# The end of a two-layer recurrent and attention kernel, put in another order

## The chip, the cores and the metric

The program runs on one core of a Trainium2 chip. A core has a matrix engine (PE; its weight loads are shown apart as PEld), a vector engine (DVE), an activation engine (ACT), a general engine (POOL), a queue engine (SP) and 16 DMA engines that they share. Every engine works through its own instructions strictly in the order in which the program holds them, and waits on semaphores for the others. The metric is the device time of one execution in microseconds (us); a smaller time is better. The program is the same for every input, so there are no data-dependent loops.

## The reference, cut to what matters

All arrays are float32. The input x has 8 batches of 512 tokens with 128 channels.

```python
xn = layernorm(x)
s  = L0_attn(xn)     # state-space scan (256 channels, 16 states), MLP with gelu, two rmsnorms
g  = silu(L0_ffn(xn))  # 24 experts, top 2 of 24, capacity 86, two layers, layernorm
x  = x + s * g       # called x1 below
xn = layernorm(x)
s  = L1_attn(xn)     # causal softmax attention, 8 heads of 128, per batch
g  = silu(L1_ffn(xn))  # 128 experts of 128x128, top 2, capacity 32 over ALL tokens
return x + s * g
```

Two things of it set the end of the program. The capacity of an expert of the second layer is counted over all 4096 tokens in order, so that the slots of the last batch are known only when its x1 is known, and the combined outputs are fetched by row numbers that the routing worked out. And `s * g` needs, for a batch, both the sum over its 8 heads and the experts' rows of its tokens.

## The kernel before, in words

The kernel is one Python function that records instructions for a scheduling layer. The layer gives each recorded instruction a place in its engine's list: an instruction that was recorded earlier goes first where it is ready in the layer's own plan of the run, and a later one may be pulled ahead of it. Buffers come from named pools with a fixed number of slots; a tile takes a slot of its tag when an older tile of that tag is done with, and slots are handed out in the order of recording. The order on each engine is therefore fixed when the program is built, and it need not be the order of the Python code.

Work of the first layer: `mixture` (24 experts, two passes) runs beside the first part of `model`, which is the state-space layer, batch after batch. `scan` (L651) is its inner part: per two states and half of the channels a product, two scans and a product on DVE (L665, L667, L668), fed by exponentials on ACT (L663), and eight transposes on PE (L689) that add into `py`. `back` (L723) ends a batch: gated output, projection, `rms`, transposes L745, gelu MLP (L751, L752, L756), second `rms`, and a store of the batch's s to DRAM (L763). 64 `step`s make up `model`.

Work of the second layer, per batch b:
- `fetch(b)` (L578) loads xn, s (L583) and x and adds two gathered rows of the first layer's experts per token;
- `after(b)` (L598) makes x1 from them: a layernorm, four elementwise operations (L605, L606, L608, L609, on POOL but for batch 0) and a store (L610);
- `prepare(b)` (L810) normalises x1 and makes `xaT`, the transposed input of attention;
- `choose(b)` and `route(b)` (L832, L856) make the logits, the top 2 and the slots, and scatter the batch's rows to DRAM in 8 indirect DMAs on POOL (L896);
- `heads(b)` (L962) yields after each of the 8 heads: `probabilities` of the next head (q product L914, four score products L922, masked minimum on DVE L924, exponential on ACT L928) and then `values` of this one (transposes L942, copies L944, products with v L949, and the scaled sums on DVE, L954 and L960). `values_of` (L900) makes v for four heads.

64 heads are to be done. 48 of them (EARLY = 6 batches) are recorded beside `model`, in one loop that advances both at the same pace, with `fetch`, `after`, `prepare` and `choose` of batch b+1 at heads 1, 3 and 4 of batch b. They share a PSUM pool of two slots, tag "pm", with `model`.

What follows is the end. The pools of the model are closed, new PSUM pools are opened (`ps_x`, `ps_q`), and a second Attention object works on them. `after`, `prepare` and `choose` of batch 7 are recorded, then `weights2` and `places` (which need the routing of all batches), and then a loop over the 16 heads of batches 6 and 7 with other work between them:

```python
    for _ in late():
        for f in second.pop(0) if second else []:
            f()
```

`second` holds the second layer's experts, 8 parts of 16 experts (`slots` loads and transposes the scattered rows, L1022 and L1025; `experts` multiplies, L1041, and stores, L1043 and L1044), one part beside a head, and then one `finish` beside each further head. `load_experts` (L1032) has eight buffers. `finish(b)` (L1046) loads the sum of the heads and x1 back from DRAM, gathers two rows per token from the experts' outputs (`gather`, 8 indirect DMAs of 128 rows per batch, six row buffers), weights and adds them on DVE (L1058, L1059), applies silu on ACT (L1060), multiplies, adds (L1061, L1062) and stores the output (L1063). No gather can start before the last expert's rows are stored, because every row of the table may be fetched.

Of the kernel before, what the change touches and what calls it, by code (L numbers as in the profile page):

```python
# [47 lines left out]
def tile_kernel(ctx: ExitStack, tc: tile.TileContext, t: dict, out: bass.AP):  # L48
# [528 lines left out]

    def fetch(b):  # L578
# [3 lines left out]
        sb = af.tile([P, NJ, D], F32, name="sb")  # L582
        Q.dma_start(sb, rows(s_dram[b][:, :]))  # L583
# [139 lines left out]
    def back(b, yt):  # L723
# [39 lines left out]
        Q.dma_start(rows(s_dram[b][:, :]), xo)  # L763
# [38 lines left out]
    class Attention:  # L802
# [129 lines left out]
        def values(self, hd, prob, v, s1):  # L932
# [12 lines left out]
            for i0 in range(0, NJ, 2):  # L945
# [9 lines left out]
                for i in range(i0, i0 + 2):  # L955
                    so, r = s1[:, i, :], rs[:, i - i0 : i - i0 + 1]
                    if hd == 0:
                        V.tensor_scalar(so, po[:, i - i0, 0:D], r, None, ALU.mult)
                    else:
                        V.scalar_tensor_tensor(so, po[:, i - i0, 0:D], r, so, ALU.mult, ALU.add)  # L960
# [71 lines left out]
    def load_experts(e0):  # L1032
        we = mo.tile([P, 8, D], F32, name="we3", bufs=8)
# [12 lines left out]
    def finish(b):  # L1046
        s1 = mo.tile([P, NJ, D], F32, name="s1f")
        Q.dma_start(s1, rows(s1_dram[b][:, :]))
        x1 = mo.tile([P, NJ, D], F32, name="x1f")
        Q.dma_start(x1, rows(x1_dram[b][:, :]))  # L1050
        y = mo.tile([P, NJ, D], F32, name="y", tag="y")
        for j in range(NJ):
            i = b * NJ + j
            ya = mo.tile([P, D], F32, name="ya", tag="row", bufs=6)
            yc = mo.tile([P, D], F32, name="yc", tag="row", bufs=6)
# [3 lines left out]
            V.scalar_tensor_tensor(y[:, j, :], yc, w121[:, i, 1:2], ya, ALU.mult, ALU.add)  # L1059
# [18 lines left out]
    def model():  # L1078
# [6 lines left out]
        for b in range(B):  # L1085
# [9 lines left out]
            for k in range(DS // NC):  # L1095
# [7 lines left out]
                if k == 6:  # L1103
# [44 lines left out]
    beside = Attention(at, m_qk, w_vo, pm, pm, (ps_s, "ps"), (ps_t, "pt"), (ps_o, "po"))  # L1148

    EARLY = 6  # L1150

    xb = after(0, *got)
    step()
    ready = {0: beside.prepare(0, xb)}
    step()

    def early():
        for b in range(EARLY):
            for hd, _ in enumerate(beside.heads(b, ready[b])):
                if hd == 0 and b == 0:  # L1160
                    beside.choose(0)
                if hd == 1:
                    got = fetch(b + 1)
                if hd == 3:
# [129 lines left out]
```

## Time and profile before

Three runs took 1581.38, 1583.21 and 1586.12 us. The profiled execution took 1584.26 us, with 1582.6 us between its first and last instruction. Stages of its end, times from the start of that span:

| us | what ends it | PE busy | DVE busy | ACT busy | POOL busy |
|---|---|---|---|---|---|
| 1296.0 to 1343.8 | transposes L745 of the last batch's `back` start | 41.2 of 47.8 | 29.4 | 23.1 | 8.1 |
| 1343.8 to 1359.5 | s of batch 7 is stored (L763) | 14.2 of 15.7 | 4.7 | 8.2 | 1.3 |
| 1359.5 to 1419.4 | first expert product (L1041) | 56.2 of 59.9 | 41.5 | 36.3 | 10.5 |
| 1419.4 to 1469.4 | last expert rows leave (L1044) | 45.9 of 50.0 | 27.8 | 14.3 | 0.0 |
| 1469.4 to 1572.9 | sum of batch 7's heads is stored (L977) | 62.6 of 103.5 | 50.5 | 45.1 | 61.8 |
| 1572.9 to 1582.6 | end | 0.0 of 9.7 | 1.4 | 0.0 | 0.0 |

A row is read as: in this stretch the engine executed something for so many us. An engine near the length of the stretch sets its pace; where none is near, the engines wait for each other or for DMAs. Over the whole span PE is busy 77% and DVE 78%; from 850 to 1300 us DVE is busy 95% of the time.

### The profile page before, as it was taken

The numbers are of one execution on the slowest core, as the hardware profiler recorded it, in microseconds if no ns is written. First come the engines' busy times: TensorE is split into PE (matmuls) and PEld (weight loads), VectorE is DVE, ScalarE is ACT, GpSimd is POOL, SyncE is SP. The second block draws the span as 40 slices with busy tenths as digits, with TensorE's granted clock in tenths as the row PEclk, the third lists the DMA queues.
The fourth block names the chain that finished last, engine by engine and source line by source line (L and its number), as shares of the span: only waits on it lengthen the run. The fifth ranks groups of instructions, "written<-read, shape, count | busy, mean of one in ns | idle before, by whom it ended". The sixth has DMA issues, their size and how long they took to land.

```text
span 1582.6 us, 20556 instructions
## 1 busy us (share of the span) xinstructions
PE 1223.6 (77%) x6793; PEld 859.4 (54%) x6793; DVE 1238.0 (78%) x2789; ACT 972.1 (61%) x1670; POOL 590.2 (37%) x501
## 2 busy tenths in 40 slices
PE   6878898213479898457998998789799898998655
PEld 4534454113367777444576755655566576567434
DVE  5687677788946867888899999999899985575454
ACT  5356776675648676565768578477575764642352
POOL 1166562656155433664343025252500302020564
PEclk9689899655689999777999999999999899999876
DMA  6577677777477764543132223232311200529233
GB/s 182 184 225 265 227 240 248 239 246 225 142 216 224 223 207 142 141 110 88 57 99 68 79 84 81 78 87 58 85 63 54 94 8 20 154 71 255 71 100 90
DMA packets 170220, 218.83 MB, mean 138 GB/s; under 512 B 16618, under 2 KB 117562, under 8 KB 170114
## 3 DMA queue, kind: packets, MB, share of 16 engines
q1 hardware_dynamic: 126018, 99.39, 20.5%
q10 hardware_dynamic: 18432, 67.12, 12.5%
q0 software_dynamic: 25664, 51.01, 12.0%
q8 instruction: 54, 0.88, 0.2%
q14 instruction: 52, 0.43, 0.1%
HBM read 161.56 MB, written 55.84 MB: 137 GB/s over the span
## 4 chain that ended last, share of the span: by engine, by line
DVE 37%; PE 29%; issue 10%; DMA 9%; ACT 7%; POOL 5%; another core or an unknown queue 2%; SPq 1%; DVEq 0%; ACTq 0%; POOLq 0%
DVE u L667 11%; DVE u L668 5%; PE po L949 4%; DVE u L665 4%; PE sc L922 4%; DVE sc L924 3%; PE py L689 2%; PE po L574 2%; DMA hd<-hs_dram,row 2%; PE pp L942 2%; DVE s L960 2%; PE ph L505 2%; PE pc L621 2%; POOL o L132 2%
## 5 line engine op out<-in xcount | busy, mean ns | idle before, releaser
L667 DVE TENSOR_TENSOR_SCAN u<-da,u 128x512 f32<-128x512 f32 x256 | 310.2, 1233 | 63.5 <-ACT da L663 54.6
L689 PE MATMUL py<-ident,u 128*128 128x128 f32 x1024 | 164.1, 301 | 158.1 <-DVE u L668 156.4
L689 PEld LDWEIGHTS py<-ident,u 128*128 128x128 f32 x1024 | 130.5, 155 | 203.5 <-DVE u L668 184.4
L949 PE MATMUL po<-v,pT 128*128 128x129 f32 x1280 | 188.1, 291 | 20.3 <-DVE s L960 11.4
L922 PE MATMUL sc<-xaT,qm 128*128 128x128 f32 (+3 forms) x512 | 182.0, 462 | 26.3 <-ACT prob L928 24.6
L663 ACT ACTIVATE da<-dt,a_neg 128x512 f32<-128x512 f32 x256 | 176.8, 720 | 38.9 <-DVE u L667 33.1
L949 PEld LDWEIGHTS po<-v,pT 128*128 128x128 f32 x1280 | 170.9, 203 | 53.0 <-issue 31.6
L928 ACT ACTIVATE prob<-sc,mn 128x128 f32<-128x128 f32 (+3 forms) x256 | 130.4, 527 | 99.3 <-DVE mn L924 82.5
L665 DVE TENSOR_TENSOR u<-bb,lp 128x1024 f32<-128x1024 f32 x128 | 154.5, 1229 | 13.8 <-DMA bb<-xd_dram 9.8
L668 DVE TENSOR_TENSOR u<-u,cb 128x1024 f32<-128x1024 f32 x128 | 156.2, 1220 | 1.2
L924 DVE CUSTOM_DVE_ANT_0 sc<-sc,mask 128x128 f32<-128x128 f32 (+3 forms) x256 | 124.3, 495 | 34.7 <-PE sc L922 28.0
L942 PE MATMUL pp<-ident,prob 128*128 128x128 f32 x640 | 113.1, 288 | 43.0 <-DVE pT L944 22.1
L942 PEld LDWEIGHTS pp<-ident,prob 128*128 128x128 f32 x640 | 80.3, 147 | 100.6 <-issue 44.6
L132 POOL DMA_INDIRECT o<-os_dram,row x60 | 103.3, 1722 | 79.6 <-DMA o<-xn_dram 32.8
L896 POOL DMA_INDIRECT xs_dram<-xn,idx x64 | 79.1, 1236 | 129.8 <-DVE row L893 50.8
L129 POOL DMA_INDIRECT xg<-xn_dram,inv x72 | 97.0, 1347 | 80.5 <-PE px L498 48.9
L129 POOL DMA_INDIRECT hg<-hid_dram,inv x72 | 89.8, 1247 | 99.5 <-PE pht L569 72.3
L922 PEld LDWEIGHTS sc<-xaT,qm 128*128 128x128 f32 x512 | 83.0, 196 | 68.8 <-ACT prob L928 43.9
L129 POOL DMA_INDIRECT hd<-hs_dram,row x64 | 80.0, 1249 | 72.0 <-DMA qkv_w<-in_qkv_w 23.8
L944 ACT COPY pT<-pp 128x384 f32<-128x384 f32 (+1 forms) x105 | 54.0, 514 | 70.9 <-PE pp L942 49.6
L574 PEld LDWEIGHTS po<-we,hgT 128*128 128x128 f32 (+1 forms) x576 | 72.5, 191 | 25.4 <-issue 20.5
L574 PE MATMUL po<-we,hgT 128*128 128x128 f32 (+1 forms) x576 | 81.2, 289 | 1.9 <-ACT hgT L571 1.8
(307 smaller groups left out, 2518.6 us busy)
## 6 DMA issues: line engine op xcount, KB each, us to landing
bb<-xd_dram ACTq DMA_DIRECT2D x64, 512.0 KB
cb<-xd_dram ACTq DMA_DIRECT2D x64, 512.0 KB
we<-in_W SPq DMA_DIRECT2D x48, 256.0 KB
hs_dram<-hs SPq DMA_DIRECT2D x24, 512.0 KB
hid_dram<-hd SPq DMA_DIRECT2D x32, 256.0 KB
we<-in_we SPq DMA_DIRECT2D x16, 512.0 KB
hs_dram<-hs SPq DMA_DIRECT2D x24, 192.0 KB
xb<-in_x SPq DMA_DIRECT2D x16, 256.0 KB
```

The lines of the kernel that those rows point to most:

```text
L129: G.indirect_dma_start(dst, None, table[:, :], IOA(idx, 0))
L132: G.indirect_dma_start(dst, None, table[:, :], IOA(idx, 0), compute_op=ALU.add)
L574: T.matmul(po[:r, c, :], hT[:, f, :r], we[:, f, :], start=False, stop=(f == NJ - 1))
L663: S.activation(da[:, j, :], dt[:, hf, :], AF.Exp, scale=a_neg[:, hf, n0 + j : n0 + j + 1])
L665: V.tensor_tensor(u, bb, bc(dx[:, hf : hf + 1, :], (P, NC, L)), ALU.mult)
L667: V.tensor_tensor_scan(u[:, j, :], da[:, j, :], u[:, j, :], 0.0, ALU.mult, ALU.add)
L668: V.tensor_tensor(u, u, cb, ALU.mult)
L689: T.matmul(py[:, i, hf * P : (hf + 1) * P], us[hf][:, j, i * P : (i + 1) * P], ident, is_transpose=True, start=False, stop=(n0 + j == DS - ...
L922: T.matmul(sc[:, :w], qm[:, i * P : w], xaT[:, :w], start=True, stop=True)
L924: V.tensor_tensor_reduce(sc[:, :w], sc[:, :w], mask[:, L - w :], -1.0, FMAX, ALU.add, ALU.min, mn[:, i : i + 1])
L942: T.transpose(pp[:, c, :], prob[i][:, k * P : (k + 1) * P], ident)
L949: T.matmul(po[:, i - i0, :], pT[:, i * (i + 1) // 2 + k, :], v[:, k, hd % 4, :], start=(k == 0), stop=(k == i),)
```

## The change

Seven edits, all of the end or leading to it.

1. 46 instead of 48 heads are recorded beside the model (`MODEL`), all by one generator over all 64 heads and with one Attention object, whose pools are replaced later.
2. `fetch(6)`, `after(6)`, `prepare(6)` and `choose(6)` move to heads 0, 1 and 2 of batch 5, and `fetch(7)` to its head 4, without s.
3. s of batch 7 is not stored and loaded again: the tile stays in SBUF (`last_s`), and L608 and L609 of batch 7, with L605 and L606, run on DVE in place of POOL.
4. `after`, `prepare` and `choose` of batch 7 are recorded right after the model, still in the model's pools; then six heads (`FILL`, numbers 46 to 51 counted from 0); then the pools are changed.
5. All 8 parts of the experts are recorded in one go; `load_experts` has six buffers in place of eight.
6. `finish` is split: `begin_finish` records loads and gathers with buffers for three batches; the weighting follows. The 12 heads left are recorded with a `finish` after each from the third on; the weighting is held behind the latest head's sums (`follows`). For batches 6 and 7 the load of the heads' sum stays in the second half.
7. The gate of the last batch's state-space output is computed at step 2 of its 8 steps, not at step 6.

```diff
@@ fetch, after, back @@
+    last_s = []
-        sb = af.tile([P, NJ, D], F32, name="sb")
-        Q.dma_start(sb, rows(s_dram[b][:, :]))
+        sb = None
+        if b < B - 1:
+            sb = af.tile([P, NJ, D], F32, name="sb")
+            Q.dma_start(sb, rows(s_dram[b][:, :]))
...
-        E = G
+        E = V if b in (0, B - 1) else G
         if o2 is not None:
-            E = V
             V.tensor_tensor(o, o, o2, ALU.add)
+        sb = last_s[0] if sb is None else sb
...
-        Q.dma_start(rows(s_dram[b][:, :]), xo)
+        if b < B - 1:
+            Q.dma_start(rows(s_dram[b][:, :]), xo)
+        else:
+            last_s.append(xo)
@@ values: both forms of the scaled sum are kept as self.summed @@
@@ load_experts @@
-        we = mo.tile([P, 8, D], F32, name="we3", bufs=8)
+        we = mo.tile([P, 8, D], F32, name="we3", bufs=6)
@@ finish @@
+    def begin_finish(b):
+        s1 = mo.tile([P, NJ, D], F32, name="s1f", bufs=3)
+        if b < B - 2:
+            Q.dma_start(s1, rows(s1_dram[b][:, :]))
+        x1 = mo.tile([P, NJ, D], F32, name="x1f", bufs=3)
+        Q.dma_start(x1, rows(x1_dram[b][:, :]))
+        yr = mo.tile([P, NJ, 2, D], F32, name="yr", bufs=3)
+        for j in range(NJ):
+            for k in range(2):
+                gather(yr[:, j, k, :], yb_dram, row1[:, b * NJ + j, k : k + 1])
+        return s1, x1, yr
+
+    def finish(b, s1, x1, yr):
+        if b >= B - 2:
+            Q.dma_start(s1, rows(s1_dram[b][:, :]))
...
-            gather(ya, yb_dram, row1[:, i, 0:1])
-            gather(yc, yb_dram, row1[:, i, 1:2])
-            V.tensor_scalar(ya, ya, w121[:, i, 0:1], None, ALU.mult)
-            V.scalar_tensor_tensor(y[:, j, :], yc, w121[:, i, 1:2], ya, ALU.mult, ALU.add)
+            ya = yr[:, j, 0, :]
+            weighted = V.tensor_scalar(ya, ya, w121[:, i, 0:1], None, ALU.mult)
+            follows(weighted, att.summed)
+            V.scalar_tensor_tensor(y[:, j, :], yr[:, j, 1, :], w121[:, i, 1:2], ya, ALU.mult, ALU.add)
@@ model @@
-                if k == 6:
+                if k == (6 if b < B - 1 else 2):
                     zsb = gate(xT)
@@ heads beside the model @@
     EARLY = 6
+    MODEL = 8 * EARLY - 2
+    FILL = 6
...
+    def all_heads():
+        for b in range(B):
+            late = b == EARLY - 1
+            for hd, _ in enumerate(att.heads(b, ready[b])):
...
+                if b < EARLY:
+                    if hd == (0 if late else 1):
+                        got = fetch(b + 1)
+                    if hd == (1 if late else 3):
+                        xb = after(b + 1, *got)
+                    if hd == (2 if late else 4):
+                        ready[b + 1] = att.prepare(b + 1, xb)
+                        att.choose(b + 1)
+                    if hd == 4 and late:
+                        last_got.append(fetch(B - 1))
...
     for _ in model_steps:
         pass
-    for _ in attention_steps:
-        pass
+    ready[B - 1] = att.prepare(B - 1, after(B - 1, *last_got[0]))
+    att.choose(B - 1)
+    for i in range(FILL):
+        next(attention_steps)
     psc.close()
     ssm.close()
@@ the end @@
-    for b in range(EARLY + 1, B):
-        ready[b] = last.prepare(b, after(b, *fetch(b)))
-        last.choose(b)
...
+    slots(0)
+    for t16 in range(E1 // 16):
+        for e0 in (16 * t16, 16 * t16 + 8):
             if e0 + 32 < E1:
                 loaded[e0 + 32] = load_experts(e0 + 32)
             experts(e0, loaded[e0])
...
         if t16 + 1 < E1 // 16:
-            second[-1].append(lambda t16=t16: slots(t16 + 1))
...
+            slots(t16 + 1)
+
+    begun = [begin_finish(b) for b in range(3)]
+    for i, _ in enumerate(attention_steps):
+        if 2 <= i < B + 1:
+            finish(i - 2, *begun[i - 2])
+            if i + 1 < B:
+                begun.append(begin_finish(i + 1))
+    finish(B - 1, *begun[B - 1])
```

More of the change, by code (lines that the diff above doesn't have):

```diff
@@ L957, in values @@
                     if hd == 0:
[L958 removed]
+                        self.summed = V.tensor_scalar(so, po[:, i - i0, 0:D], r, None, ALU.mult)
                     else:
[L960 removed]
+                        self.summed = V.scalar_tensor_tensor(so, po[:, i - i0, 0:D], r, so, ALU.mult, ALU.add)
         def heads(self, b, xaT):
```

49 lines of the change are left out of this document (8 added, 41 removed).

## The prediction

> **What bounds the kernel now.** I read, in this order, the table of stretches, the waits of the last stage, the order in time of SP and POOL around the last batch, and then, for each engine, the order in which the built program issues its instructions, before and after. Stretches of before (start:end, length, busy us and instructions of PE, PEld, DVE, ACT, POOL, granted clock, DMA share, GB/s):
>
> ```profile
> 1296.00:1343.80 47.80, 41.15 (x265) 31.69 (x263) 29.43 (x108) 23.07 (x47) 8.07 (x10) 1.00 0.04 12
> 1343.80:1359.50 15.70, 14.16 (x55) 7.61 (x56) 4.72 (x13) 8.19 (x18) 1.26 (x1) 1.00 0.07 18
> 1359.50:1419.40 59.90, 56.22 (x309) 38.17 (x307) 41.52 (x176) 36.30 (x68) 10.52 (x11) 1.00 0.49 130
> 1419.40:1469.40 50.00, 45.93 (x436) 36.44 (x436) 27.78 (x67) 14.34 (x27) 0.00 (x0) 0.97 0.82 230
> 1469.40:1572.90 103.50, 62.63 (x273) 45.35 (x271) 50.52 (x176) 45.10 (x68) 61.75 (x64) 0.77 0.31 89
> ```
>
> Up to 1469 PE is the bound, 92 to 94% busy from 1359 on: the chain of the last batch costs nothing there, because heads fill it. From 1469 nothing is busy over 61%. That stage is a convoy of 64 gathers, whose waits are:
>
> ```profile
> POOL ya L129 <- DMA yb_dram<-yb: 59.6, 1, 59.6
> ACT prob L928 <- DVE mn L924: 20.7, 5, 7.3
> DVE rsum L954 <- remote: 19.3, 3, 8.6
> PEld sc L922 <- ACT prob L928: 16.2, 4, 7.8
> POOL ya L129 <- DVE y L1059: 9.0, 4, 5.7
> ```
>
> The first line is POOL idle for 59.6 us until the last expert row is stored. Then it issues a gather each 1.25 us; the first starts 3.1 us after the last store (1469.4 to 1472.5). The chain of the last batch, SP first, then POOL:
>
> ```profile
> 1359.45 0.36 SPq L763 DMA_DIRECT2D s_dram<-xnb  x1
> 1361.90 3.96 SPq L1034 DMA_DIRECT2D we<-in_we  x4
> 1365.90 1.74 SPq L583 DMA_DIRECT2D sb<-s_dram  x1
> ...
> 1572.93 0.36 SPq L977 DMA_DIRECT2D s_dram<-s  x1
> 1575.22 0.36 SPq L1048 DMA_DIRECT2D s1f<-s_dram  x1
> 1579.27 0.38 SPq L1063 DMA_DIRECT2D out<-y  x1
> ```
>
> ```profile
> 1372.38 1.27 POOL L608 TENSOR_TENSOR o<-o,sb 128x512 f32<-128x512 f32 x1 [26.15 <-DMA sb<-s_dram]
> 1373.73 1.27 POOL L609 TENSOR_TENSOR xb<-o,xb 128x512 f32<-128x512 f32 x1
> 1402.64 1.01 POOL L896 DMA_INDIRECT xs_dram<-xn,idx  x1 [27.64 <-DVE idx L890]
> ```
>
> s goes out at 1359.45, its reload is issued behind four weight loads and lands at 1372.38, x1 is ready at 1375.0, the slots at 1402.6, the scatters end at 1412.9.
>
> **A price list for PE**, in us per instruction of the program, from rows such as fourteen L949 records (seven instructions) in 1.73 and 32 L1041 records (16) in 1.90: L949 0.25, L942 0.155, L922 0.63 (mean of four widths), L914 and L907 1.0, L1025 0.15, L1041 0.119; one head 8.6. Multiplied with the order of before it gives 76.7 for 1343.8 to 1419.4 (75.6 measured) and 46.5 for the experts (50.0 measured, the rest waits for rows). So it may be used on the order of after.
>
> **1. Up to the last batch's `back` (L745; 1343.8 before).** 47 heads instead of 48 lie in front of it on PE, 7.6 us less by the list; DVE has 8.1 us less before L740. The new order has 17 more activation-table loads on ACT (85 for 68 up to the last exponential of the scan), 1.283 us each in the rows, 21.8 us. ACT is idle about 30% there, so they cost between 0 and 8 us (what is saved elsewhere); I take 2, since only 13.0 us of DVE's idle time from 1000 to 1296 came from ACT's L663. Other orders have shifted DVE's idle time by some us in 50 (0.4 to 7.1 by window), bounds -4 and +4. L745 starts at 1338. The gate's early place removes 2.2 us from PE here, inside the 7.6 already; it is covered by the same PE work that fills the stage.
>
> **2. s kept.** The `back` itself stays 15.7 long: 1353.7. Then L608 and L609 run on DVE; the like 128x512 product L1061 takes 0.68, together 1.4, x1 at 1355.1. Before, this took 15.6 (1359.4 to 1375.0), so 14.2 is saved on the chain. The store of the eighth batch's s and its reload fall away on SP; nothing waited behind them but the weight loads, which are early anyway. Bounds: 1.3 (two times 0.66) and 2.5 (POOL's two at 1.27).
>
> **3. The chain runs bare.** In the order of after PE goes from L756 straight through L826, L838, L843, L870, L880 and L881 to L1010, and only then come heads; DVE likewise has no head between L721 and L893. The heads that were to fill the chain use q products in the same two-slot PSUM tag as the chain, recorded after it. So PE, which was 94% busy here, does only the 14.4 us of L745 to L1010. Length of the chain without heads, from the rows: statistics and roots 3.9 with L117, L823 0.68, transposes and copies to the logits 3.8, maxima and indices 2.8, subtract, exponential (with a table load) and masks 4.3, counts and the first products 1.8: heads resume on PE after about 19.5, at 1374.6; the slots are ready after 22 (27.6 before, with heads between). Bounds 17 (no semaphore gap) and 27.6. Idle PE: some 21 us. On POOL a memset of v (L904), which waits for the 48th head's last product, now stands in front of the eighth scatter: it ends near 1390 instead of 1388. On SP the sum of batch 5's heads (the same head) is stored in front of the first row loads. Both are covered by the heads that PE has to do before it can use the rows; without that cover they would cost some 2 us.
>
> **4. Heads before the experts.** On PE 24 L922, 50 L942, 43 L949, 8 L907, 6 L914 and 8 L1025 stand before the first L1041: 49.0 by the list. The first head has no other beside it, and the clock has to come back: 4 more (0 to 7). The first expert product is at 1427.6 (1419.4 before), with 51.3 heads done instead of 54. A row bears on the clock: it was 1.00 where PE was 90% busy and 0.77 where it was 61%. [...]
>
> **5. Experts in one go.** 128 L1041, 56 L1025 and 3.6 heads' work: 47.8 by the list, times 50.0/46.5, is 51.4. Six weight buffers leave ten loads of 512 KB for this stage, eight before, while DMA share was 0.82; 0 to 5, I take 0, since the first rows and six weights can land while PE is with the heads. Last rows leave at 1479.0, first gather 1482.1. Ten us late.
>
> **6. Gathers.** Three batches may now be in flight, so POOL should not wait for L1059 (9.0) again: batch 6 is complete 55 x 1.25 + 2.5 (a gather's landing) = 71.2 after the first, at 1553.3. A weighting that waits for its gather holds back all minima behind it on DVE, and through them ACT's exponentials and PE's transposes. In DVE's order batch 6's weighting stands in front of the scores and sums of the last 2.5 to 3 heads. Until then DVE needs five heads (5.0 each: minima 2.5, sums 1.6, copies 0.9) and six finishes (3.8 each) in 60 us, 80%, where it was 49%; a slip of 5 (0 to 16) is taken. After it PE has 17.2 by the list, at least; 20 with the last head's latency. Last sum at 1578.3. On SP the store of batch 6's head sums stands in front of the loads for batch 3's finish; it waits for head 56, some 14 us after the rows leave, and batch 3's gathers end 30 us later: covered. The end from there is the same as before, 9.7 (store, reload, two DVE operations, output): 1588.0.
>
> **Sum.** 1338 + 15.7 + 1.4 + 19.5 + 53.0 + 51.4 + 3.1 + 71.2 + 5 + 20 + 9.7 = 1588.0, against a span of 1582.6. The profiled run took 1584.26 and the median of the runs is 1583.21, so the span is 0.6 under the median: I forecast 1589. No change is anything within 0.3%, 4.7 us, which is about what a measurement of this kernel can tell.
>
> **Rivals.**
> - Faster, 1573: the new end holds more work beside the gathers, and it pays. If the chain takes 17, PE runs by the list without the 4 and the 3.6 us of expert waits, and the slip is 0, the rows leave at 1467 to 1470 and the end is 106 later. For it: up to 1469 PE has 19.6 us less list work than before, and the chain is 20 us shorter. Against: 21 us of PE idle. It decides when the rows leave before 1471, or the slip is 0 and they leave before 1474.
> - The same, 1583: half of these gains arrive; the new idle of PE in the chain and the old idle in the gather stage (40.9 before) exchange places.
> - Much slower, 1600: the convoy stays. Outputs of batches 0 to 6 left 12.4 us apart before (1490.2 to 1564.9); at that pace, with more heads, batch 6 is 15 later than by gathers alone.
>
> **How the numbers follow.** Forecast (1584 to 1597 for itself) 0.42, faster 0.27, same 0.18, much slower 0.13. Most of the first is past 0.3%: faster 0.28, same 0.21, slower 0.51. The range 1570 to 1603 leaves about one in ten on each side: the low end takes the faster rival's bounds, the high end the convoy.
>
> **What would show it.** Right: PE nearly idle for 20 us after the last L756; no L949 between L761 and L893; x1 under 2 us after the last L721; the first L1041 after 1422; gathers without pauses; the last L960 some 20 us after batch 6's L1059. Wrong: heads inside the chain, the rows of the experts leaving before 1470, or POOL waiting again for L1059. A changed pace between 830 and 1300 us, where the order differs too, would shift everything.

## The result, and the profile after

The changed kernel takes 1624.87 us (median of four runs, 1619.21 to 1627.04) where the kernel before takes 1582.68 (four runs): the ratio is 1.0258, 95% interval 1.0225 to 1.0290. It is slower, as forecast, but by 42 us where I had 6 (1589 against 1583), and the time lies outside my range (1570 to 1603). The profiled execution took 1619.21 us, its span is 1617.5.

First the table of stretches of the changed kernel (start:end, length, busy us and instructions of PE, PEld, DVE, ACT, POOL, granted clock, DMA share, GB/s):

```profile
1343.00:1358.60 15.60, 8.18 (x42) 5.15 (x41) 4.14 (x12) 7.48 (x16) 1.26 (x1) 0.92 0.00 0
1358.60:1425.40 66.80, 55.09 (x254) 35.19 (x254) 39.91 (x154) 28.46 (x55) 7.83 (x9) 0.81 0.39 103
1425.40:1474.70 49.30, 45.53 (x451) 36.68 (x451) 28.05 (x70) 14.62 (x28) 0.13 (x1) 1.00 0.89 246
1474.70:1607.30 132.60, 78.40 (x361) 52.64 (x359) 61.34 (x206) 53.06 (x81) 62.03 (x64) 0.79 0.25 70
```

The last `back` (L749 now), the chain with the six heads behind it, the experts, and the stage behind the last expert rows. The last stretch is the news: 132.6 us instead of 103.5, with PE busy for 78.4 instead of 62.6. No engine is busy over 60% in it, as before. Against the terms of my sum, each read from the starts of the named instructions:

| term | forecast | measured |
|---|---|---|
| start of the last L749 (L745 before) | 1338 | 1342.6 |
| from there to x1 | 17.1 | 16.0 |
| to the heads on PE | 19.5 | 15.0 |
| to the first expert product | 53.0 | 51.8 |
| to the last expert rows | 51.4 | 49.3 |
| to the first gather | 3.1 | 3.0 |
| to the last head sum | 96.2 | 129.6 |
| the end from there | 9.7 | 10.2 |

Seven terms together are 3.9 us shorter than forecast. The eighth is 33.4 us too long, and it is the whole miss. (The profiled execution is 5.7 us under the median of the runs.) The waits in it:

```profile
POOL yr L129 <- DMA yb_dram<-yb: 49.8, 1, 49.8
ACT pT L951 <- remote: 30.5, 1, 30.5
PEld po L956 <- issue: 27.5, 9, 14.3
POOL yr L129 <- DVE y L1074: 19.7, 2, 11.7
DVE rsum L961 <- remote: 14.9, 1, 14.9
DVE pT L951 <- remote: 11.5, 2, 6.3
```

The first line is POOL's wait for the experts. The others are new in size. "remote" is a wait that ended without a releaser that the profile knows; ACT (L951 copies transposed scores out of PSUM) stood in one for 30.5 us in one piece. DVE and then PE in order of time show what lies around it (start, length, line and operation, and in brackets the idle time before it and what ended that):

```profile
1503.44 0.69 DVE L915 COPY v<-pv 128x512 f32<-128x512 f32 x1 [1.27 <-issue]
1510.44 0.56 DVE L951 COPY pT<-pp 128x384 f32<-128x384 f32 x1 [6.31 <-remote]
1510.92 0.68 DVE L1076 TENSOR_TENSOR y<-y,s1f 128x512 f32<-128x512 f32 x1
1526.54 0.17 DVE L961 RECIPROCAL rsum<-po 128x2 f32<-128x2 f32 x1 [14.94 <-remote]
1526.63 0.67 DVE L1077 TENSOR_TENSOR y<-y,x1f 128x512 f32<-128x512 f32 x1
...
1532.86 0.69 DVE L915 COPY v<-pv 128x512 f32<-128x512 f32 x1 [5.03 <-remote]
1534.31 0.57 DVE L931 CUSTOM_DVE_ANT_0 sc<-sc,mask 128x384 f32<-128x384 f32 x1 [0.76 <-remote]
```

```profile
1501.93 0.87 PE L949 MATMUL pp<-ident,prob 128*128 128x128 f32 x3 [5.26 <-DVE mn L931]
1502.59 1.50 PE L956 MATMUL po<-v,pT 128*128 128x129 f32 x6
1504.19 2.08 PE L914 MATMUL pv<-w_vo,xaT 128*128 128x512 f32 x2
1511.06 1.12 PE L949 MATMUL pp<-ident,prob 128*128 128x128 f32 x4 [4.79 <-issue]
1511.97 3.19 PE L929 MATMUL sc<-xaT,qm 128*128 128x384 f32 x4
1527.97 1.63 PE L956 MATMUL po<-v,pT 128*128 128x129 f32 x6 [12.80 <-issue]
```

They have to be read in pairs. DVE's reciprocal at 1526.54 needs the products po that PE shows at 1502.59 to 1504.09, and DVE was free from 1511.6 on. Its copy of v at 1532.86 needs the products pv of 1504.19 to 1506.27, and its minimum at 1534.31 the scores that PE shows from 1511.97. ACT's copy of pT, the 30.5 us wait, needs the transposes of 1511.06 and starts at 1534.27. So the engines behind PE start 20 to 27 us after the records of what they wait for have ended. In the trace's log of PE's own semaphore there is no entry for 16 us before 1526.52, and then, at 1534.24, 1534.28 and 1534.33, three within 0.1 us, while the products that they report (1511.06 to 1515.16) are recorded 0.8 us and more apart. This log lacks some 6% of its entries, so the starts of DVE and ACT are the firmer evidence; both say the same. PE's results were there and were reported late. Meanwhile POOL gathers:

```profile
1527.73 0.95 POOL L129 DMA_INDIRECT yr<-yb_dram,row  x1 [0.30 <-issue]
1540.37 0.95 POOL L129 DMA_INDIRECT yr<-yb_dram,row  x1 [11.70 <-DVE y L1074]
...
1559.63 0.94 POOL L129 DMA_INDIRECT yr<-yb_dram,row  x1 [0.30 <-issue]
1568.58 0.95 POOL L129 DMA_INDIRECT yr<-yb_dram,row  x1 [8.00 <-DVE y L1074]
```

The first line ends a run of 40 gathers without a pause, from 1477.73; runs of 16 and of 8 follow. No head was completed between 1483.9 and 1538.3: the next one came 54 us later, when POOL had stopped.

**A measure.** For each of the 704 instructions of DVE and ACT that take a head's result from PE (minima, reciprocals, copies of q, v and pT) I take the time from the end of PE's record to the start of the taker, but no more than the taker's engine had stood idle. I call it lateness. (A wait for a free buffer is in it too, so a few us of it need not be a late report.) Before the gather stage none of it is over 2 us in the two traces. In the gather stage of the kernel before it goes up to 8.6 us, in the changed kernel to 22.1.

### The profile page after: what moved, and what is told of

Its sections match the earlier page's. It is cut to its first block, busy times and chain, and to the rows that moved or that the text cites. A ratio compares the mean times of both kernels' runs of the same rounds, so it can differ in the third digit from the quotient of the medians.

```text
span 1617.5 us, 20550 instructions
## 1 busy us (share of the span) xinstructions
PE 1223.0 (76%) x6793; PEld 853.2 (53%) x6793; DVE 1243.8 (77%) x2792; ACT 991.1 (61%) x1684; POOL 584.8 (36%) x497
## 3 DMA queue, kind: packets, MB, share of 16 engines
q0 software_dynamic: 25664, 51.01, 11.9%
## 4 chain that ended last, share of the span: by engine, by line
DVE 35%; PE 29%; DMA 10%; issue 8%; ACT 8%; POOL 5%; another core or an unknown queue 3%; SPq 1%; ACTq 0%; DVEq 0%; POOLq 0%
DVE u L671 10%; DVE u L672 5%; PE sc L929 4%; PE po L956 4%; DVE u L669 3%; DVE sc L931 3%; PE py L693 2%; PE pp L949 2%; DMA bb<-xd_dram 2%; PE pqm L921 2%; POOL o L132 2%; PE pv L914 2%; PE po L574 2%; PE ph L505 2%
## 5 line engine op out<-in xcount | busy, mean ns | idle before, releaser
L956 PE MATMUL po<-v,pT 128*128 128x129 f32 x1280 | 183.8, 286 | 46.7 <-DVE s L967 23.3
L956 PEld LDWEIGHTS po<-v,pT 128*128 128x128 f32 x1280 | 167.0, 199 | 78.9 <-issue 49.8
L949 PE MATMUL pp<-ident,prob 128*128 128x128 f32 x640 | 111.8, 284 | 38.2 <-DVE pT L951 16.1
L132 POOL DMA_INDIRECT o<-os_dram,row x60 | 105.0, 1750 | 80.7 <-DMA o<-xn_dram 33.8
L949 PEld LDWEIGHTS pp<-ident,prob 128*128 128x128 f32 x640 | 78.1, 144 | 100.4 <-issue 45.5
L903 POOL DMA_INDIRECT xs_dram<-xn,idx x64 | 74.8, 1169 | 146.4 <-DVE row L900 105.0
L951 ACT COPY pT<-pp 128x384 f32<-128x384 f32 (+1 forms) x100 | 51.7, 517 | 85.4 <-PE pp L949 47.2
L129 POOL DMA_INDIRECT yr<-yb_dram,row x64 | 62.0, 969 | 88.6 <-DMA yb_dram<-yb 49.8
L574 PEld LDWEIGHTS po<-we,hgT 128*128 128x128 f32 (+1 forms) x576 | 72.1, 190 | 24.2 <-issue 19.4
```

The source lines that it names most:

```text
L129: G.indirect_dma_start(dst, None, table[:, :], IOA(idx, 0))
L132: G.indirect_dma_start(dst, None, table[:, :], IOA(idx, 0), compute_op=ALU.add)
L949: T.transpose(pp[:, c, :], prob[i][:, k * P : (k + 1) * P], ident)
L956: T.matmul(po[:, i - i0, :], pT[:, i * (i + 1) // 2 + k, :], v[:, k, hd % 4, :], start=(k == 0), stop=(k == i),)
```

## The experiments

One thing has to be known ahead of them. The runs fell on several chips, and these are of two kinds. On the first kind the kernel before takes 1582 to 1590 us, and every kernel with gathers shows lateness in this stage. On the second kind it takes 1552 to 1553, and lateness is 4.3 us at most and mostly none; in the log of PE's semaphore no entry stands more than 0.03 us behind its instruction's end, from start to end of all eight traces. So ratios are to the kernel before on the same chip, and "rows" is the time from the last L749 to the last expert rows, "stage" the time from there to the last head sum. Times are those of the profiled execution, ratios those of the runs; where no interval stands there was one run.

| kernel | chip kind | ratio to before | rows | stage | lateness: largest, sum |
|---|---|---|---|---|---|
| before, first trace | 1 | 1 | 124.5 | 103.5 | 8.6, 36 |
| b_same | 1 | 1.0001 (0.9976 to 1.0027) | 129.9 | 107.2 | 13.9, 30 |
| b_rows24 | 1 | 1.009 | 129.6 | 116.7 | 33.8, 84 |
| b_rows24_same | 1 | 1.0086 (1.0053 to 1.0119) | 130.6 | 119.4 | 32.4, 92 |
| changed, first trace | 1 | 1.0258 (1.0225 to 1.0290) | 131.4 | 132.6 | 22.1, 59 |
| a_same | 1 | 1.0270 (1.0232 to 1.0308) | 131.5 | 133.7 | 22.1, 61 |
| a_again | 1 | 1.0273 (1.0221 to 1.0325) | 131.3 | 139.1 | 22.1, 69 |
| a_row6_same | 1 | 1.0167 (1.0118 to 1.0216) | 132.2 | 125.1 | 8.0, 50 |
| a_plain_pool | 1 | 0.992 | 135.8 | 76.5 | 0.7, 0 |
| a_pace | 1 | 1.023 | 131.6 | 136.4 | 24.2, 72 |
| a_unread | 1 | 1.003 | 133.4 | 92.8 | 3.3, 17 |
| a_late_fill3_2 | 1 | 1.0125 (1.007 to 1.018) | 115.8 | 127.6 | 13.3, 53 |
| a_pace8 | 2 | 1.033 | 130.6 | 114.8 | 4.3, 4 |
| a_yr1 | 2 | 1.020 | 130.6 | 109.6 | 3.0, 3 |
| a_row6 | 2 | 1.015 | 132.3 | 98.4 | 2.1, 2 |
| a_late | 2 | 1.0074 (1.0043 to 1.0105) | 130.2 | 80.9 | 0.7, 0 |
| a_fill3 | 2 | 1.0076 (1.0046 to 1.0106) | 114.7 | 98.8 | 1.4, 0 |
| a_late_fill3 | 2 | 0.9958 (0.9928 to 0.9987) | 115.2 | 81.9 | 0.7, 0 |
| b_plain_pool | 2 | 0.988 | 135.4 | 51.8 | 2.1, 2 |
| b_keep_s | 2 | 0.9980 (0.9957 to 1.0003) | 120.0 | 93.4 | 0.1, 0 |

(The sum adds what is over 1.5 us on DVE and ACT, which partly lie beside each other. In b_plain_pool lateness is counted from the first transfer on, which lies ahead of the stage.)

**Is it the gathers, or the waiting for them?** Theory A: POOL's gathers themselves make PE's reports late. Theory B: order, since DVE waits for rows in front of the heads' minima.

a_plain_pool, in `begin_finish`:

```
-gather(yr[:, j, k, :], yb_dram, row1[:, b * NJ + j, k : k + 1])
+i = (b * NJ + j) * 2 + k
+G.dma_start(yr[:, j, k, :], yb_dram[P * i : P * (i + 1), :])
```

> The changed kernel with the 64 gathers of the finishes replaced by 64 plain transfers of 64 KB issued on POOL's own queue; it leaves out the choice of rows (each finish gets consecutive rows of yb_dram, so its values are others). All waits stay. Theory A (the runs of gathers themselves hold back what PE reports to DVE and ACT): in the stage from the first transfer to the last head sum no DVE or ACT instruction starts more than 4 us after the PE instruction that it waits for has ended (in the changed kernel up to 27 us), the stage takes 95 to 105 us instead of 130, and the whole some 1590 (1583 to 1600). Theory B (the delay is order: the weighting of a batch stands on DVE in front of the heads' minima and waits for its transfers): POOL issues at about the same pace, so the stage stays over 115 us and the whole over 1610.

1570.8 us against 1584.2 of before, less than the 1583 to 1600 of theory A, and a lateness of 0.7 us at most. Its size is not only that: the plain transfers of the first rows need not wait for the last experts and began at 1437.6, so the stage is shorter for a second reason. What follows is that without gathers the reports come in time. The same execution holds a counterpart: its first layer still fetches rows by indirect gathers, 15 of them without a pause from 425.95 on. There a result of PE (its row first, from the order of PE; then ACT's) came 7.7 us late:

```profile
438.51 1.11 PE L574 MATMUL po<-we,hgT 128*128 128x128 f32 x8
...
447.28 0.37 ACT L575 ACTIVATE os<-po,wsl 128x128 f32<-128x128 f32 x1 [6.89 <-remote]
```

All twelve traces of the first kind have such a wait between 410 and 460 us, of 3.2 to 11.9 us; the eight of the second kind have not one "remote" wait on DVE or ACT.

a_unread:

```
+sink = mo.tile([P, NJ, 2, D], F32, name="sink", bufs=1)
 for j in range(NJ):
     for k in range(2):
-        gather(yr[:, j, k, :], yb_dram, row1[:, b * NJ + j, k : k + 1])
+        gather(sink[:, j, k, :], yb_dram, row1[:, b * NJ + j, k : k + 1])
+Q.dma_start(yr.rearrange("p j k d -> p (j k) d"), rows(yb_dram[2 * b * L : 2 * (b + 1) * L, :]))
```

> The changed kernel, all 64 gathers kept, but into a tile that nobody reads; the finishes work on consecutive rows that one plain transfer per batch brings (so the choice of rows is left out of the values). No engine waits for a gather any more, and POOL runs all 64 without a pause. Theory A: PE's results still reach DVE and ACT late, by over 10 us somewhere in the run of gathers; the stage from the first gather to the last head sum takes 110 to 140 us, the whole 1600 to 1630. Theory B: with nobody waiting for a gather the stage falls to 85 to 95 us and the whole to 1570 to 1585.

1589.2 us, stage 92.8. Neither theory had it: the stage lies in B's range, the whole 4 us above it and 11 under A's. Lateness is there without any engine waiting for a gather, but it is 3.3 us at most, not over 10, and 17 us in all instead of 59. The run was also not what I expected of it. `sink` has one buffer, so POOL waited for its own landings and issued in eights, with pauses of 2.2 to 5.9 us between them. So a wait for gathers is not needed for late reports; whether they are smaller here for the pauses, or cost less since nobody waits, the run cannot tell.

**Does the length of a run matter?** a_pace was to put pauses between the gathers:

```
+pause = mo.tile([P, NJ, D], F32, name="pause", bufs=1)
+for _ in range(4):
+    G.memset(pause, 0.0)
```

> The changed kernel with four fills of a 128x512 tile on POOL behind each eight gathers (a pause of some 2 to 5 us for what a gather does, without a wait for another engine). Theory A: lateness ends in each pause, so none is over 10 us, and the stage takes 105 to 118 us instead of 130, the whole 1597 to 1612, although the gathers themselves come later. Theory B: gathers that come later make the weightings later and with them the heads: the stage takes 130 to 150, the whole 1625 to 1645.

It failed as an experiment: nothing tied the fills to the gathers, and the scheduler put all 32 at 1356 to 1374, 0.525 us each. What ran was the changed kernel again, 1621.35 us, 1.023 of before, with a lateness of 24.2.

b_rows24, in the kernel before:

```
-we = mo.tile([P, 8, D], F32, name="we3", bufs=8)
+we = mo.tile([P, 8, D], F32, name="we3", bufs=6)
...
-ya = mo.tile([P, D], F32, name="ya", tag="row", bufs=6)
-yc = mo.tile([P, D], F32, name="yc", tag="row", bufs=6)
+ya = mo.tile([P, D], F32, name="ya", tag="row", bufs=24)
+yc = mo.tile([P, D], F32, name="yc", tag="row", bufs=24)
```

> The kernel before with 24 row buffers for the gathers instead of 6 (and six weight buffers instead of eight, as the changed kernel has): POOL no longer pauses for the weightings. Theory A: longer runs of gathers, PE's results late by over 10 us, the stage from the first gather to the last head sum 110 to 125 us instead of 100, the whole 1592 to 1608. Theory B: buffers that come free earlier can only help: 1575 to 1583.

1599.16 us against 1584.23. More buffers made the kernel before slower, and its largest lateness four times as long (33.8 against 8.6), with runs of 40, 16 and 8 gathers where the kernel before has none over 22. It was repeated with intervals below. (The weight buffers changed with the rows'. They act before the last rows leave, and in the repetition, from the last L745 on, 12 of the 13 us that it lost to b_same lie behind the last rows.)

a_pace8, the pauses tied in order:

```
...
-gather(yr[:, j, k, :], yb_dram, row1[:, b * NJ + j, k : k + 1])
+g = G.indirect_dma_start(yr[:, j, k, :], None, yb_dram[:, :], IOA(row1[:, b * NJ + j, k : k + 1], 0))
+if paced[0] is not None:
+    follows(g, paced[0])
+paced[0] = g
+count[0] += 1
+if count[0] % 8 == 0:
+    for _ in range(6):
+        z = G.memset(pause, 0.0)
+        follows(z, paced[0])
+        paced[0] = z
...
```

> The changed kernel with a pause on POOL behind every eight gathers: six fills of a 128x512 tile (0.525 us each, 3.15 together), now tied in order between the gathers, and no wait for another engine. Theory A (PE's results are reported late while POOL issues gathers one behind the other): lateness ends in each pause and none is over 10 us (24 to 27 without pauses); the last gather comes 22 us later than by pace alone, but the heads are no longer held: stage from first gather to last head sum 105 to 118 us, the whole 1597 to 1612. If a pause of 3 us does not clear it, lateness over 15 us stays and the whole is 1620 or more.

a_yr1:

```
-yr = mo.tile([P, NJ, 2, D], F32, name="yr", bufs=3)
+yr = mo.tile([P, NJ, 2, D], F32, name="yr", bufs=1)
```

> The changed kernel with one buffer for a batch's gathered rows instead of three, so POOL must wait for the last weighting of a batch before it gathers the next. Theory A: runs of eight gathers with pauses of 3 us and more, lateness up to 10 us, stage 110 to 125 us, the whole 1600 to 1615, faster than the changed kernel although a buffer was taken away. Theory B (order on DVE and waiting for gathers): less lookahead, so slower than 1625.

a_row6:

```
-yr = mo.tile([P, NJ, 2, D], F32, name="yr", bufs=3)
+yr = {}
 for j in range(NJ):
     for k in range(2):
-        gather(yr[:, j, k, :], yb_dram, row1[:, b * NJ + j, k : k + 1])
+        yr[j, k] = mo.tile([P, D], F32, name="yr", tag="row", bufs=6)
+        gather(yr[j, k], yb_dram, row1[:, b * NJ + j, k : k + 1])
...
-ya = yr[:, j, 0, :]
+ya = yr[j, 0]
...
```

> The changed kernel with six row buffers for the gathers, the size before, instead of 24; all else of the change stays. Theory A: POOL pauses again within each batch as before the change, lateness at most some 10 us, stage 100 to 112 us, the whole 1590 to 1602, near what I forecast for the change. Theory B: 1620 or more.

b_plain_pool, the kernel before with `G.dma_start` of consecutive rows as in a_plain_pool:

> The kernel before with its 64 gathers replaced by plain transfers of 64 KB on POOL's queue (it leaves out the choice of rows). It tells what the gathers cost before the change, and, beside the changed kernel without gathers (1570.8), what the rest of the change is worth. Theory A: no lateness, some 15 to 30 us of the 100 us stage go: 1553 to 1568; the rest of the change then costs 3 to 18 us. If it takes 1575 or more, the gathers cost the kernel before next to nothing and the rest of the change is a gain that they hide.

All four ran on a chip of the second kind, where the kernel before took 1553.49. They took 1605.33, 1585.23, 1577.42 and 1534.48. Lateness was 4.3 us at most, whatever the pauses, so these runs could not tell what they were made for. They told two other things. Pauses where there is nothing to cure only cost: 3.3% over before with them, where I estimate 1.8% without (below). And on a chip without lateness the changed kernel with six buffers is still 1.5% slower than before. The plain transfers in the kernel before gained 19 us; they too began early, at 1418.5.

**Both buffer counts in both kernels, on one chip** (first kind). b_same and a_same are the two kernels unchanged, the others the two edits of buffers above.

> The kernel before itself, unchanged, for its trace and time on the same chip as the three others of this group, since stretches of the same program came out 10 to 15 us apart on two chips. Both theories: within 0.3% of the kernel before; the stage from the last expert rows to the last head sum 95 to 105 us.

> The changed kernel, unchanged, on the same chip as the others of this group. Both theories: 2.2 to 2.9% over before, the stage 125 to 135 us, lateness over 20 us.

> The changed kernel with six row buffers for the gathers instead of 24, on the same chip as the changed kernel. Theory A (runs of gathers without pause delay PE's reports): 25 to 40 us faster than the changed kernel, 1.000 to 1.010 of before; that rest is what my sum had (1.004). Theory C (the slowness is the plan, 78 us of PE work behind the expert rows, whatever the buffers): less than 10 us faster than the changed kernel, 1.018 to 1.026 of before.

> The kernel before with 24 row buffers and six weight buffers, on the same chip. Theory A: 8 to 18 us slower than before (1.005 to 1.012), lateness over 10 us against less than 10 in before. Theory C: same as before within 0.3%.

They took 1588.52, 1632.74, 1618.25 and 1605.6 us. 24 buffers cost 0.9% in the kernel before and 1.0% in the changed one; the rest of the change costs 1.7 to 1.8% with either. Neither theory was right alone: A had wanted 1.000 to 1.010 for a_row6_same and it is 1.0167, C had wanted at least 1.018. The largest lateness on this kind of chip goes with the longest run of gathers without a pause: 3.3 us with runs of 8 (a_unread), 8.0 to 13.9 with 22 or 24 (both kernels with six buffers, a_late_fill3_2 below), 22.1 to 33.8 with 40. The waits of b_rows24_same show the buffers' part, on the two engines that take from PE:

```profile
POOL ya L129 <- DMA yb_dram<-yb: 64.2, 1, 64.2
DVE rsum L954 <- remote: 41.0, 2, 33.2
ACT v L908 <- remote: 28.4, 1, 28.4
```

**The remaining 1.7%: order on DVE, and PE idle in the chain.** a_late moves the weightings:

```
-if 2 <= i < B + 1:
-    finish(i - 2, *begun[i - 2])
-    if i + 1 < B:
-        begun.append(begin_finish(i + 1))
+if 4 <= i < B + 4 - 1:
+    finish(i - 4, *begun[i - 4])
+    if i - 4 + 3 < B:
+        begun.append(begin_finish(i - 4 + 3))
```

> The changed kernel with each batch's weightings recorded two heads later (finish of batch i-4 instead of i-2 behind the i-th head), all 24 row buffers and the gathers' pace kept. Theory B (DVE waits for gathers in front of the heads' minima, and from there all other engines): by then the rows have landed, so the stage from the last expert rows to the last head sum falls from 133 to 95 to 108 us and the time to 1.000 to 1.010 of before. Theory A (gathers without a pause delay PE's reports by themselves, whoever waits): the stage stays over 118 us, the time over 1.016.

a_fill3 moves heads:

```
+for i in range(3):
+    next(attention_steps)
 ready[B - 1] = att.prepare(B - 1, after(B - 1, *last_got[0]))
 att.choose(B - 1)
-for i in range(FILL):
+for i in range(FILL - 3):
     next(attention_steps)
```

> The changed kernel with three of the six heads recorded in front of the chain of the last batch instead of all six behind it: PE, idle for 20 us in the chain, does 2.5 to 3 heads there. Expected by both theories: the last expert rows leave 12 to 20 us earlier against the last product of the last batch's back (131 us after it in the changed kernel, so 111 to 119), the stage behind stays 125 to 136 us, the time 1.015 to 1.020 of before. If the idle PE of the chain cost nothing: 1.024 to 1.030.

a_late_fill3 is both:

> Both edits together: weightings two heads later and three heads in the chain. If theory B holds and the two costs add: 0.985 to 1.000 of before, faster than both kernels. Theory A: 1.005 to 1.016.

These ran on a chip of the second kind: 1561.77, 1560.13 and 1546.53 us, against 1551.91 of before. There is no lateness there, so they cannot decide between the theories, and a_fill3 missed what I expected of it (stage 125 to 136, 1.015 to 1.020). a_fill3 has the changed kernel's order of DVE behind the experts, instruction for instruction, and its stage takes 98.8; with the weightings later it takes 80.9 (a_late) and 81.9 (both). So on this kind of chip the order alone cost 17 to 18 us, with no lateness in it. Stretches of a_fill3 and of a_late_fill3, the chain with heads and the last stage each:

```profile
1348.50:1400.80 52.30, 46.48 (x252) 31.47 (x251) 37.52 (x153) 30.31 (x55) 7.83 (x9) 1.00 0.52 140
...
1447.80:1546.60 98.80, 73.97 (x362) 50.47 (x360) 61.12 (x208) 53.04 (x81) 62.54 (x64) 0.90 0.33 94
```

```profile
1355.50:1407.80 52.30, 46.49 (x254) 31.51 (x253) 37.47 (x153) 30.27 (x54) 7.82 (x9) 1.00 0.52 141
...
1455.20:1537.10 81.90, 68.38 (x362) 47.94 (x360) 59.48 (x206) 50.87 (x81) 59.69 (x62) 0.96 0.38 107
```

The first line of each is the filled chain. From x1, 1.7 us into it, to the first expert product it takes 50.6 us where the bare one takes 66.8, at full clock instead of 0.81. Rows leave 15.5 us earlier after the last L749 than in a_late on the same chip (114.7 for 130.2), inside the 12 to 20 that I gave. In the second line of a_late_fill3 PE is busy for 83% of the stage (59% in the changed kernel). Together the two edits make 0.9958 of before: on this kind of chip a version that is faster than before by 0.4% (0.1 to 0.7). The changed kernel itself was not run there.

b_keep_s, one part of the change alone in the kernel before:

```
-Q.dma_start(rows(s_dram[b][:, :]), xo)
+if b < B - 1:
+    Q.dma_start(rows(s_dram[b][:, :]), xo)
+else:
+    last_s.append(xo)
...
+if sb is None:
+    E, sb = V, last_s[0]
...
+xb_last = after(B - 1, *fetch(B - 1))
 psc.close()
 ssm.close()
```

> The kernel before with one part of the change alone: s of the last batch is kept in its tile instead of stored and loaded back, and the two products behind it run on DVE. The chain is some 14 us shorter. My reading of before (the chain costs nothing there, since heads fill PE, 92 to 94% busy): the same within 0.5%, 0.995 to 1.005. Rival (the chain sets the experts' start and with it the end): 0.988 to 0.993.

1549.24 us, 0.9980 (0.9957 to 1.0003): the same. (With it x1 of the last batch is recorded ahead of the change of pools.) No trace of the kernel before is from this kind of chip, so its traces of the first kind have to serve. Counted from the last L745, the last scatter came after 52 us instead of 67 (the first trace of before; 68.5 in b_same), so the chain was 15 us shorter, as I had said (14.2), and its first expert product came 16 us earlier (21 against b_same); the rows left only 4.5 us earlier (10 against b_same). PE did more of the heads between the experts: 102 records of products with v (L958 there, L949 before) in that stretch instead of 60.

**The same pair on a chip of the first kind.**

> The changed kernel once more, beside the next one, since PE's reports came late in every kernel with gathers on the chips where the kernel before takes some 1585 us, and in none on those where it takes some 1552. If this chip takes 1585 for before: 1.022 to 1.031, lateness over 20 us. If it takes 1552: no lateness over 3 us with the engine idle, the stage 95 to 108 us instead of 133, and 1.012 to 1.020 of before, the rest being the chain without heads.

> The changed kernel with weightings two heads later and three heads in the chain, on the same chip as the changed kernel. On a chip that takes 1552 for before: 0.993 to 0.999 again, and 1.5 to 2.5% under the changed kernel. On one that takes 1585: if the lateness needs engines that wait for gathers, none over 10 us and 0.985 to 0.998; if POOL's gathers cause it by themselves, lateness over 15 us and 1.003 to 1.015.

1633.31 and 1606.35 us against 1586.91. The best version is 1.0125 of before here: still 27 us better than the changed kernel (15.5 of it before the rows leave, 11.5 in the stage), but lateness is back, although the weightings stand late. By time this is in the range of theory A, but the lateness, 13.3, is between what the two had. Its waits in the stage:

```profile
ACT prob L935 <- DVE mn L931: 37.7, 4, 15.9
DVE rsum L961 <- remote: 21.3, 3, 13.3
...
PEld po L956 <- remote: 15.4, 2, 9.1
```

## Why the prediction was wrong

**The steps that held.** The price list for PE, made from the order of before, held for the order of after: 53.0 (4 of it for the clock) and 51.4 forecast, 51.8 and 49.3 measured. One sum in it does not fit its words: 3.6 whole heads at 8.6 would make 54.6 of step 5, not 47.8; for what PE did execute there the list gives 49. L745 was to start at 1338 and started at 1342.6, but in the two traces of the kernel before and the two of b_rows24, all on the first kind of chip, that start lies anywhere from 1333.8 to 1351.9, so this miss tells nothing. The bare chain: x1 1.6 us after the last L721, L725 now (under 2), heads on PE at 1373.6 (1374.6 forecast), the memset of v in front of the eighth scatter, which started at 1393.39. The kept s saves some 15 us on the chain and nothing clear of noise at the end, which b_keep_s shows by itself. The first expert product at 1425.4 (1427.6), the first gather at 1477.7 (1482.1).

**The clock after the idle chain** I priced at 4 us by the rows. The stretches are

```profile
1358.60:1373.60 15.00, 4.05 (x16) 3.35 (x16) 8.95 (x45) 3.94 (x7) 0.00 (x0) 0.50 1.05 275
1373.60:1390.00 16.40, 15.87 (x55) 8.41 (x55) 11.00 (x41) 4.48 (x9) 5.78 (x6) 0.70 0.28 74
```

A clock of 0.70 over 16.4 us is 4.9 us lost. It stood at 0.50 for the first 9.8 us of the heads' work (1373.6 to 1383.4, PE 9.27 us busy) and at 1.00 from there on. So the loss is 0.9 over the 4, inside the 0 to 7 that I gave.

**The step that failed is the sixth: "a slip of 5 (0 to 16) is taken", and with it "POOL should not wait".** Its three pieces, with what the changed kernel took, and a_fill3, which has the same order on DVE but ran on a chip without lateness (the landing taken at 2.5 us behind a gather's start, as in the forecast):

| piece of the stage | forecast | changed | a_fill3 |
|---|---|---|---|
| first gather until batch 6's rows have landed | 71.2 | 84.4 | 73.5 |
| slip, to the end of batch 6's weighting | 5 | 25.9 | 0.6 |
| from there to the last head sum | 20 | 19.3 | 21.6 |

The slip was 20.9 us short, outside of its own bounds, and the gathers 13.2, of which 11.7 is one wait of POOL. The end of the weighting in the changed kernel is that of this line:

```profile
1587.40 0.61 DVE L1074 SCALAR_TENSOR_TENSOR y<-yr,w 128x128 f32<-128x128 f32 x2
```

What stood in their place is late reports, a cost that my sum had put at nothing: heads stood still, the weightings stand behind them on DVE, and POOL waits for the weightings. In the changed kernel's chain that ended last, two pieces have no known releaser:

```profile
1503.81 30.47 another core or an unknown queue
1550.95 5.17 another core or an unknown queue
```

35.6 us without a name, about as much as the 33.4 that were missed. And such lines stand in the chain of before, which I had on the table:

```profile
1495.30 8.63 another core or an unknown queue
...
1515.93 5.51 another core or an unknown queue
...
1535.73 5.14 another core or an unknown queue
...
1564.91 4.39 another core or an unknown queue
```

23.7 us. The program runs on one core and has no queue that I did not know, so these lines were a cost without a name, a quarter of the stage. I showed "DVE rsum L954 <- remote: 19.3" and drew nothing from it. My sum for the stage after was made bottom up, from prices, and so held none of it; the time before, with which I compared, held all of it. Carried over unchanged in place of the slip, it would have made 1588 + 18.7 = 1607 of the forecast, an estimate that still falls 10 us short of the span.

**"Three batches may now be in flight, so POOL should not wait for L1059 (9.0) again"** was wrong here: POOL waited 19.7 us for L1074. And the pauses that I counted as a loss of before were worth something: with 6 buffers, so with shorter runs, both kernels are faster than with 24, by 0.9 to 1.0%, 14 to 17 us.

**"A weighting that waits for its gather holds back all minima behind it on DVE"** was right, and its price was in the sum, as the 20 us behind batch 6's weighting: 19.3 and 21.6 measured. What I did not see is that it can be avoided. In a_late_fill3 the last head sum comes 5.2 us after that weighting, and the stage is 16.9 us shorter than in a_fill3.

**Without lateness** my stage was right, as a sum (99.3 us forecast from the last rows to the last head sum, 98.8 in a_fill3) and nearly in its pieces. The changed kernel itself was not run on such a chip. From a_fill3's 1.0076 and the 15.5 us that its chain saves, of 1552, I estimate 1.018 for it there, 1580 us, which is near my 1589. But the kernel before is some 30 us faster on such a chip, so even there the ratio of 1.004 would have been too low.

**The rivals.** "The convoy stays", 1600, had the right mechanism, gathers and heads holding each other up, at less than half its price (15 of 33). "Faster, 1573" needed a stage of 106 from the last rows to the end; it exists, 93 us, in a_late and a_late_fill3, without lateness and with the weightings two heads later.

**What stays open.** That gathers on POOL bring PE's late reports is shown: none in the stage without gathers, some in every kernel with them, on that kind of chip, and both in one execution (a_plain_pool). What carries it in the chip is not, nor why it is in one kind of chip and not in the other. One rival of a different sort stands untested: that the recording of the profile has a part in it. In all twelve traces of the first kind the logs of PE, DVE and ACT lack 3 to 10% of the entries that their instructions should have left, in the eight of the second kind next to none, and a granted clock was recorded in every execution, so none is known to have run without recording. How the loss divides between late reports and order on the first kind is not shown either: no run has six buffers, the later weightings and the filled chain together. That pauses between gathers help was not tried by itself: a_pace8 fell on the other kind of chip, and a_unread, which had pauses, also had nobody waiting.

## What to carry to other kernels

A wait without a known releaser in the profile of before is a cost that a sum from prices does not contain: carry it over as a term of its own, or leave it out of the time that you compare with. A buffer count that paces a queue can be worth its pauses; more lookahead for indirect gathers made both kernels slower here, by 0.9 to 1.0%, on the first kind of chip. And order the work that waits for transfers behind work that does not, on the in-order engine that both share: that, and three heads in an idle chain, were worth 27 us together on a chip of the first kind (1633.31 to 1606.35). Where no report is late I estimate 32 to 34 (16.9 or 17.9, and 15.5), more than the 28 that the change is estimated to cost there.

## What the runs showed of the hardware

PE's results were reported to DVE and ACT up to 33.8 us late (b_rows24) while POOL issued indirect gathers one behind the other, on the chips of the first kind; on the second the same measure gives 4.3 us at most. From DVE to ACT there was no such thing: in the traces of before and of the changed kernel the exponentials that had to wait started 0.04 us or less after the minimum, in the same stages. On the second kind of chip no entry in the log of PE's semaphore stands more than 0.03 us behind its instruction's end; the 22.1 us of the changed kernel are of another order, and no run shows what makes them. It has to be said against my measure that the profile models PE's ends (its records overlap: the transposes from 1511.06 end at 1512.18, the scores start at 1511.97); the three reports within 0.1 us and the starts of DVE and ACT do not rest on them.

In the changed kernel PE's clock stayed at 0.50 for 9.8 us of nearly unbroken work (9.27 us busy) after an idle chain of 15 us with PE busy for 4.05, and went to 1.00 then.

One chip differs from another by 2% for the same program (1552 and 1585 us for the kernel before), and the ratio of two kernels differs with it: 0.9958 and 1.0125 for the same version. A ratio from one chip is a statement on that chip.
